# Two of sixteen attention-weight tiles of a unit made by GpSimd instead of VectorE, in a four-layer graph network

## The chip, the cores and the metric

The kernel runs on one core of one Trainium2 chip. The metric is the device time of one execution in microseconds (us), of which the median over runs is given. The engines are named as the profile names them: PE is TensorE (matrix products), DVE is VectorE, ACT is ScalarE, POOL is GpSimd, and SP is the queue from which most transfers (DMAs) are issued.

## The reference

Eight graphs (`x`: 8 x 2048 nodes x 64 features) share one adjacency matrix `adj` of 2048 x 2048. Four layers follow one another, each inside a residual with a layer norm. The first three are graph attention:

```
h   = x @ W                      # layer 0 has a layer norm and node weights ahead of it
s1  = h @ a[:64];  s2 = h @ a[64:]
e   = leaky_relu(s1[i] + s2[j], slope 0.2)
att = softmax over j of e, where adj[i, j] > 0
x   = layernorm(x + act(att @ h))      # act: elu in layers 0 and 1, relu in layer 2
```

Layer 3 is a softmax over neighbours for each feature and has no share in the change.

## The kernel before, in words

**Units.** The work of one layer on one graph is a unit. Line 1328 fixes the order: layer 0 of graphs 0 to 3, layer 1 of graphs 0 to 3, then the same for graphs 4 to 7, and then layer 2 of all eight. So units 0 to 15 belong to the first two layers. The text numbers units in that order.

**Tiles.** A unit has 16 tiles, one for every 128 source nodes j. A tile `w` has 128 partitions (j) and 2048 columns (all target nodes i), in float32. In layers 0 and 1 the exponential of the leaky score needs no ScalarE: with e^(0.8 s1[i]) as a row `r` over i and e^(-0.8 s2[j]) as a column `e[:, 1]`, the tile is

```
w[:, sl] = max(r[:, sl], low[:, jb]) * edge[:, jb, sl]
```

which is one VectorE instruction (`weights`, line 920). `edge` is the mask, kept in SBUF as FP8. `r` is the same row on all 128 partitions. Unit 0 has it in SBUF. For all later units TensorE spreads it into PSUM (`spread`, line 767) from three bfloat16 pieces `r3`, since PSUM holds one `r` only: the next unit's `r` can be written when VectorE has read the last tile of the present one. The first and last tile of such a unit are made in two halves.

`products` (line 969) multiplies each tile by the values `v` of its 128 nodes, four matmuls of 512 columns (two instructions each), and sums into PSUM over the 16 tiles. There are four `w` buffers, and one set of sums, which ScalarE copies out (`oT`) at the end of a unit.

**Order.** The loop over units and their 16 tiles is written out. Everything on TensorE, VectorE, ScalarE and GpSimd keeps program order (`InOrder`, line 70), and each engine executes its own queue strictly in that order. At tile (step) jb of a unit the loop emits: the weights (`reach`, line 949), the products, from step 10 on what prepares the next unit (`prepare`, line 747), and one step of each background generator (`Streams`, line 1294). Transfers are ordered by the framework's planner, and SP issues them one after the other.

**Background work.** While unit n runs, generators finish the unit before it and prepare later ones:

- `finish` (line 988) normalizes the sums (`den`, `p_o`), adds `hb` on GpSimd in layer 0 (called `o+hb` below), takes the elu on ScalarE, adds on GpSimd `eh<-eh,x` (`eh`) and `o<-o,eh` (`o+eh`), and then takes the statistics of the layer norm: `stats` (line 508) emits on VectorE the reduces `st_x<-o` and, two steps later, `st_x<-sq_x`; a power on GpSimd follows. At the earliest the first reduce is emitted at step 11 after a layer 0 unit and at step 9 after a layer 1 unit; `o+eh` is emitted two steps before it, `eh` three. Waits for PSUM slots can push all of these later.
- `scores` (line 698) and `features0` (line 608) make the scores of later units. Both end in `rows_term` (line 589): ScalarE copies the 8 KB row into `rT`, GpSimd splits it into three bfloat16 pieces with three casts and two in-place subtractions, and SP writes them to DRAM. `prepare` reads them back as `r3`, and multiplies `v` on GpSimd (`pv`).
- `mask_out` (line 310) widens the mask to float32 on ScalarE (`mf`, 32 copies, one every two steps from step 4 to 14, in units 9 to 14), and each copy is written to DRAM in a transfer of 512 KB. It uses four buffers, those of the integer mask's loads before it.

Of the kernel before, what the change touches and what calls it, by code (L numbers as in the profile page):

```python
# [8 lines left out]
F32 = mybir.dt.float32  # L9
F32R = mybir.dt.float32r  # L10
BF16 = mybir.dt.bfloat16
U8 = mybir.dt.uint8
FP8 = mybir.dt.float8e4
I32 = mybir.dt.int32
AF = mybir.ActivationFunctionType
ALU = mybir.AluOpType
AX = mybir.AxisListType

P = 128
# [31 lines left out]
def gnn4_kernel(ctx: ExitStack, tc: tile.TileContext, t, out):  # L51
    nc = tc.nc
    x_in, adjT = t["x"], t["adjT"]
    B, N, F = x_in.shape
    K = N // P
    K2 = K // 2
# [50 lines left out]
    class Banks:  # L107
# [7 lines left out]
        @classmethod  # L115
        def use(cls, name, bufs):
            if cls.stack is not None:
                cls.stack.close()
            cls.stack = ExitStack()
            cls.pool = cls.stack.enter_context(tc.tile_pool(name=name, bufs=bufs, space=PSUM))  # L120
# [139 lines left out]
    half_ldeg = consts.tile([P, K], F32, name="half_ldeg")  # L260
    raws = {}

    AT_W = (0, 1, 2, 3, 6, 7, 8, 9)

    def load_raw(jb):

        if jb in AT_W:
            r = work.tile([P, N], I32, tag="w", name=f"raw_{jb}", bufs=4)
            nc.sync.dma_start(r, adjT[jb * P : (jb + 1) * P])
            raws[jb] = [r[:, : N // 2], r[:, N // 2 :]]  # L270
        elif jb < K:
            raws[jb] = []
            for h in range(2):
                r = early.tile([P, N // 2], I32, tag="raw", name=f"raw_{jb}_{h}", bufs=4)
                nc.sync.dma_start(
                    r, adjT[jb * P : (jb + 1) * P, h * (N // 2) : (h + 1) * (N // 2)]
                )
                raws[jb].append(r)
# [31 lines left out]
    def mask_out():  # L310

        for jb in range(K):
            for h in range(2):
                while not 3 < now[2] < K - 1:
                    yield 1
                r = early.tile([P, K2, P], F32, tag="raw", name=f"mf_{jb}_{h}", bufs=4)
                act.copy(
                    r,
                    edge[:, jb, h * (N // 2) : (h + 1) * (N // 2)].rearrange(
                        "p (i c) -> p i c", c=P  # L320
                    ),
                )
                nc.sync.dma_start(
                    mask_d[h * K2 : (h + 1) * K2, :, jb].rearrange("i p c -> p i c"), r
                )
                yield 2
# [262 lines left out]
    def rows_term(sc, p, n, layer, b):  # L589

        if in_psum(layer, b):
            r = small.tile([K, P], F32, tag="rT", name=f"rT_{n}", bufs=1)
            act.copy(r, p)
            r3 = small.tile([K, 3, P], BF16, tag="rT3", name=f"rT3_{n}", bufs=1)
            for i in range(3):
                pool.tensor_copy(r3[:, i], r)
                if i < 2:
                    pool.tensor_tensor(r, r, r3[:, i], ALU.subtract)
            sc.row = dram.tile([3, K, P], BF16, tag="row3_d", name=f"row3_d_{n}", bufs=B + 1)
            nc.sync.dma_start(sc.row.rearrange("m k p -> k m p"), r3)  # L600
            return
        rT = small.tile([K, P], F32, tag="rT", name=f"rT_{n}", bufs=1)
        act.copy(rT, p)
        sc.row = dram.tile([K, P], F32, tag="row_d", name=f"row_d_{n}", bufs=B + 1)

        (nc.scalar if n == "0_0" else nc.sync).dma_start(sc.row, rT)
# [140 lines left out]
    def prepare(layer, b):  # L747

        n = f"{layer}_{b}"
        sc = S[layer, b]  # L750
        if in_psum(layer, b):
            sc.r3 = work.tile([P, 2 * N], BF16, tag="row", name=f"row3_{n}")[:3, :N]
            nc.sync.dma_start(sc.r3, sc.row.rearrange("m k p -> m (k p)"))
            if layer == 2:
                sc.v = V[layer, b].v
                return
            sc.v = early.tile([P, K, F], F32, tag="pv", name=f"pv_{n}", bufs=2)
            pool.tensor_tensor(sc.v, V[layer, b].v, bc_f(sc.e[:, 2]), ALU.mult)
            return
        sc.r = work.tile([P, N], F32, tag="row", name=f"row_{n}")  # L760
        (nc.scalar if n == "0_0" else nc.sync).dma_start(
            sc.r, bass.AP(tensor=sc.row.tensor, offset=sc.row.offset, ap=[[0, P], [1, N]])
        )
        sc.v = early.tile([P, K, F], F32, tag="pv", name=f"pv_{n}", bufs=2)
        pool.tensor_tensor(sc.v, V[layer, b].v, bc_f(sc.e[:, 2]), ALU.mult)

    def spread(layer, b):
# [148 lines left out]
    def halves(u, jb):  # L916
        parts = 2 if jb in (0, K - 1) and in_psum(u.layer, u.b) else 1
        return [slice(c * (N // parts), (c + 1) * (N // parts)) for c in range(parts)]

    def weights(u, jb):  # L920

        s = u.s
        w = u.w[jb] = work.tile([P, N], F32, tag="w", name=f"w_{u.n}_{jb}", bufs=4)
        low = s.low if u.layer == 2 else s.e[:, 1]
        for sl in halves(u, jb):
            dve.scalar_tensor_tensor(
                w[:, sl], s.r[:, sl], low[:, jb : jb + 1], edge[:, jb, sl], ALU.max, ALU.mult
            )
# [20 lines left out]
    def reach(t):  # L949

        while front[0] < K * len(todo):
            n, jb = divmod(front[0], K)
            layer, b = todo[n]
            if n not in prepared or front[0] > t + (2 if layer == 2 else 0):
                break
            if jb == 0:
                spread_for(n)
                units.append(unit(layer, b))
            weights(units[n], jb)
            front[0] += 1  # L960
            if jb == K - 1 and n + 1 in prepared:
                spread_for(n + 1)
        while behind[0] < min(front[0], t + 2):
            n, jb = divmod(behind[0], K)
            if todo[n][0] == 2:
                exponential(units[n], jb)
            behind[0] += 1

    def products(u, jb):

        s, w = u.s, u.w[jb]
        sums = [u.acc[c // 2][F * (c % 2) : F * (c % 2) + F, :] for c in range(NCH)]
        for c in range(NCH):
            pe.matmul(
                sums[c],
                lhsT=s.v[:, jb, :],
                rhs=w[:, c * 512 : (c + 1) * 512],
                start=(jb == 0),
                stop=False,
            )  # L980
        if jb == K - 1:

            assert s.whole
            for c in range(NCH):
                rows = slice(32 * c, 32 * c + 3)
                pe.matmul(sums[c], lhsT=s.mean[rows], rhs=emptyT[rows], start=False, stop=True)
# [384 lines left out]
    begin = {0: 2, 1: 3, 4: 4, 5: 5, 6: 6, 8: 7}  # L1371
    for n, (layer, b) in enumerate(todo):
        if (layer, b) == (2, 1):
            early_.close()
            late = ctx.enter_context(tc.tile_pool(name="late", bufs=1))
            bg.add(l3_products())
# [6 lines left out]
        for jb in range(K):  # L1383
            if n == 0:
                while masks < min(K, 9 + jb):
                    mask(p_deg, masks)
                    masks += 1
                    if masks == K:
                        empties(p_deg)
            now[2] = jb  # L1390
            reach(K * n + jb)
            u = units[n]
            if jb == 0:
# [539 lines left out]
```

## Time and profile before

| what | value |
|---|---|
| median of 3 runs | 1438.56 us (1435.73 to 1440.45) |
| profiled execution, its own time | 1439.37 us |
| its span | 1437.6 us |
| granted TensorE clock, mean | 0.945 |
| span from the end of unit 0 (115.7 us) to that of unit 15 (784.3 us) | 668.6 us |

The span runs from the first to the last instruction in the trace; times in the trace count from its start. In a group of instructions, "out<-in" names the tiles, "x" the number of instructions, then follow the busy time, the mean in ns, and the idle time of the engine just before them with what ended it. In a list of waits the three numbers are the total, the count and the longest. In a timeline the first two numbers are the start and the duration in us; a group in brackets is the idle time before, and what ended it. All instructions of the in-order engines carry the line of the recording helper (L80), so they are told apart by tile. Busy time of TensorE includes modelled ends.

### The profile page before, as it was taken

What the parts mean: (1) busy time and instruction counts of PE and PEld (TensorE: products, weight loads), DVE (VectorE), ACT (ScalarE), POOL (GpSimd) and SP (SyncE); (2) the same over time, 40 slices, a digit from 0 to 9 for tenths busy, and PEclk for the clock granted to TensorE, in tenths of its full rate; (3) what the DMA queues carried; (4) which work ended last, traced back from release to release, by engine and by line L of the source; (5) the groups of instructions that cost most, each with busy time, mean ns of one, the idle gap of its engine ahead of it and who ended that gap; (6) DMA issues with size and microseconds to landing.
All of it is one profiled execution on the core that took longest, in us unless ns stands there. A gap on an engine that the chain in (4) does not pass through costs nothing.

```text
span 1437.6 us, 19117 instructions
## 1 busy us (share of the span) xinstructions
PE 1238.5 (86%) x7138; PEld 620.0 (43%) x7138; DVE 1260.6 (88%) x1260; ACT 820.3 (57%) x1585; POOL 548.0 (38%) x619
## 2 busy tenths in 40 slices
PE   3578788988899988999998887879999898988996
PEld 2323233333233333344332332336665464647996
DVE  4699889997899999999999898898989988878976
ACT  4415444664557545654533986787677766675442
POOL 1152463324423344331322211312445534367665
PEclk9988999999999999999999897999999998989998
DMA  8740000000000022221201000005453354531111
GB/s 297 249 81 1 1 2 1 1 2 1 3 1 1 22 69 88 89 75 53 68 16 37 1 1 15 12 26 150 130 155 101 108 152 116 141 97 46 38 37 33
DMA packets 113335, 90.36 MB, mean 63 GB/s; under 512 B 58077, under 2 KB 91021, under 8 KB 112082
## 3 DMA queue, kind: packets, MB, share of 16 engines
q1 hardware_dynamic: 112690, 87.89, 20.9%
q8 instruction: 58, 0.95, 0.3%
q10 hardware_dynamic: 544, 1.17, 0.2%
q14 instruction: 43, 0.35, 0.1%
HBM read 63.54 MB, written 25.46 MB: 62 GB/s over the span
## 4 chain that ended last, share of the span: by engine, by line
PE 28%; DVE 20%; ACT 8%; issue 5%; POOL 3%; DMA 1%; SPq 0%; POOLq 0%; DVEq 0%; ACTq 0%
PE p_l L80 13%; DVE w L80 12%; PE acc L80 12%; ACT w L80 3%; DVE st_x L80 2%; ACT x L80 2%; DVE o L80 1%; PE p_o L80 1%; ACT sp L80 1%; POOL o L80 1%; PE r L80 1%; DMA mask<-mask_d 1%; DVE x L80 1%; DVE nd L80 1%; DVE fs L80 1%
## 5 line engine op out<-in xcount | busy, mean ns | idle before, releaser
L80 DVE SCALAR_TENSOR_TENSOR w<-r,se,edge 128x2048 f32<-128x2048 f32 (+1 forms) x270 | 555.4, 2103 | 22.0 <-PE r L80 19.2
L80 PE MATMUL acc<-w,pv 128*64 128x512 f32 x2048 | 508.9, 629 | 70.8 <-DVE w L80 63.9
L80 DVE SCALAR_TENSOR_TENSOR w<-r,lo_g,edge 128x2048 f32<-128x2048 f32 (+1 forms) x144 | 298.0, 2095 | 18.1 <-PE r L80 9.7
L80 PE MATMUL acc<-w,x 128*64 128x512 f32 x1024 | 269.1, 656 | 37.0 <-ACT w L80 33.0
L80 ACT ACTIVATE w<-w,down_g 128x2048 f32<-128x2048 f32 (+1 forms) x144 | 257.3, 1809 | 71.2 <-DVE w L80 70.7
L80 PEld LDWEIGHTS p_l<-v,mask 128*128 128x128 f32 x2048 | 253.0, 193 | 65.4 <-issue 52.3
L80 PEld LDWEIGHTS acc<-w,pv 128*64 128x64 f32 x2048 | 133.5, 141 | 337.3 <-issue 190.2
L80 PE MATMUL p_l<-v,mask 128*128 128x256 f32 x2048 | 269.1, 289 | 9.8 <-POOL mask L80 6.3
L80 PEld LDWEIGHTS acc<-w,x 128*64 128x64 f32 x1024 | 68.2, 146 | 163.5 <-issue 92.2
L80 ACT COPY oT<-acc 128x512 f32<-128x512 f32 x48 | 25.8, 589 | 147.5 <-PE acc L80 147.5
L80 ACT ACTIVATE x<-o,st_x 128x64 f32<-128x64 f32 x256 | 90.5, 444 | 1.4 <-DVE st_x L80 1.4
L80 ACT ACTIVATE o<-p_o,den 128x64 f32<-128x64 f32 x256 | 55.9, 326 | 44.9 <-DVE den L80 44.9
L80 ACT ACTIVATE nd<-p_l,empty 128x256 f32<-128x256 f32 x64 | 30.2, 471 | 82.5 <-PE p_l L80 82.4
L80 POOL TENSOR_SCALAR isw_x<-isw_x 128x16 f32<-128x16 f32 x24 | 6.2, 260 | 182.6 <-DVE isw_x L80 171.1
L80 POOL TENSOR_TENSOR st_x<-isw_x,mhalf 128x16 f32<-128x16 f32 x24 | 70.3, 2930 | 2.0
L80 PEld LDWEIGHTS p_o<-rh,oT 128*128 128x128 f32 x384 | 49.7, 196 | 35.9 <-issue 15.4
L80 POOL TENSOR_TENSOR st_h<-isw_h,mhalf 128x16 f32<-128x16 f32 x8 | 23.6, 2952 | 106.7 <-DVE isw_h L80 83.8
L80 PE MATMUL p_o<-rh,oT 128*128 128x130 f32 x384 | 59.9, 293 | 4.6 <-ACT o L80 3.5
L80 DVE RECIPROCAL nd<-nd 128x256 f32<-128x256 f32 x32 | 55.8, 1743 | 0.0
L80 POOL TENSOR_TENSOR eh<-eh,x 128x1024 f32<-128x1024 f32 (+2 forms) x24 | 36.4, 1532 | 45.3 <-ACT eh L80 45.2
L80 POOL COPY x<-x 128x16 f32<-128x16 f32 x16 | 3.3, 205 | 123.8 <-ACT x L80 123.8
L80 PE MATMUL r<-row,ones 3*128 3x512 bf16 x92 | 26.9, 416 | 24.7 <-DVE w L80 23.6
(243 smaller groups left out, 1497.4 us busy)
## 6 DMA issues: line engine op xcount, KB each, us to landing
mask<-mask_d SPq DMA_DIRECT2D x140, 256.0 KB
mask_d<-mf SPq DMA_DIRECT2D x32, 512.0 KB
raw<-in_adjT_dram SPq DMA_DIRECT2D x8, 1024.0 KB
raw<-in_adjT_dram SPq DMA_DIRECT2D x16, 512.0 KB
x<-in_x_dram SPq DMA_DIRECT2D x8, 512.0 KB
x_d<-x SPq DMA_DIRECT2D x8, 512.0 KB
e<-x_d SPq DMA_DIRECT2D x64, 64.0 KB
out_dram<-o SPq DMA_DIRECT2D x64, 64.0 KB
```

The source lines that it names most:

```text
L80: ins = f(*args, **kwargs)
```

## The change

For units 1 to 15, tiles 6 and 12 (`ASIDE`) are no longer made by VectorE. GpSimd makes each in four pieces of 512 columns (`aside`): a tensor_scalar with two maxima, and a multiply by the mask. One piece is emitted at the start of each of steps 1 to 4 (tile 6) and 7 to 10 (tile 12), five tiles ahead. `products` takes the pieces in place of the columns of `w`. There are four piece buffers (`off`), so a piece of tile 12 reuses the buffer of tile 6's piece of the same number.

[...]`rows_term` also writes `rT` in float32 to DRAM (8 KB), ahead of GpSimd's split, and `prepare` reads it back onto all 128 partitions (`rowf`, 1 MB, one buffer).

Memory for this comes from three places. The integer mask's buffers move to a pool of their own, closed at step 8 of unit 0, and a pool "stage" takes their place. `mf` gets one buffer there instead of four. The values `v` of units 1 to 15 move from the pool "early" to the second half of the row tile whose first half holds `r3`.

```diff
--- before.py
+++ after.py
@@ -260,6 +260,18 @@
     half_ldeg = consts.tile([P, K], F32, name="half_ldeg")
     raws = {}
 
+    class Stage:
+        stack = ExitStack()
+        pool = None
+
+        @classmethod
+        def use(cls, name):
+            cls.stack.close()
+            if name:
+                cls.pool = cls.stack.enter_context(tc.tile_pool(name=name, bufs=1))
+
+    Stage.use("raws")
+
     AT_W = (0, 1, 2, 3, 6, 7, 8, 9)
 
     def load_raw(jb):
@@ -271,7 +283,7 @@
         elif jb < K:
             raws[jb] = []
             for h in range(2):
-                r = early.tile([P, N // 2], I32, tag="raw", name=f"raw_{jb}_{h}", bufs=4)
+                r = Stage.pool.tile([P, N // 2], I32, tag="raw", name=f"raw_{jb}_{h}", bufs=4)
                 nc.sync.dma_start(
                     r, adjT[jb * P : (jb + 1) * P, h * (N // 2) : (h + 1) * (N // 2)]
                 )
@@ -313,7 +325,7 @@
             for h in range(2):
                 while not 3 < now[2] < K - 1:
                     yield 1
-                r = early.tile([P, K2, P], F32, tag="raw", name=f"mf_{jb}_{h}", bufs=4)
+                r = Stage.pool.tile([P, K2, P], F32, tag="mf", name=f"mf_{jb}_{h}", bufs=1)
                 act.copy(
                     r,
                     edge[:, jb, h * (N // 2) : (h + 1) * (N // 2)].rearrange(
@@ -591,6 +603,8 @@
         if in_psum(layer, b):
             r = small.tile([K, P], F32, tag="rT", name=f"rT_{n}", bufs=1)
             act.copy(r, p)
+            sc.rowf_d = dram.tile([K, P], F32, tag="row_d", name=f"rowf_d_{n}", bufs=B + 1)
+            nc.sync.dma_start(sc.rowf_d, r)
             r3 = small.tile([K, 3, P], BF16, tag="rT3", name=f"rT3_{n}", bufs=1)
             for i in range(3):
                 pool.tensor_copy(r3[:, i], r)
@@ -749,19 +763,25 @@
         n = f"{layer}_{b}"
         sc = S[layer, b]
         if in_psum(layer, b):
-            sc.r3 = work.tile([P, 2 * N], BF16, tag="row", name=f"row3_{n}")[:3, :N]
+            both = work.tile([P, 2 * N], BF16, tag="row", name=f"row3_{n}")
+            sc.r3 = both[:3, :N]
             nc.sync.dma_start(sc.r3, sc.row.rearrange("m k p -> m (k p)"))
             if layer == 2:
                 sc.v = V[layer, b].v
                 return
-            sc.v = early.tile([P, K, F], F32, tag="pv", name=f"pv_{n}", bufs=2)
+            sc.rowf = Stage.pool.tile([P, N], F32, tag="rowf", name=f"rowf_{n}")
+            nc.sync.dma_start(
+                sc.rowf,
+                bass.AP(tensor=sc.rowf_d.tensor, offset=sc.rowf_d.offset, ap=[[0, P], [1, N]]),
+            )
+            sc.v = both[:, N:].bitcast(F32).rearrange("p (k f) -> p k f", k=K)
             pool.tensor_tensor(sc.v, V[layer, b].v, bc_f(sc.e[:, 2]), ALU.mult)
             return
         sc.r = work.tile([P, N], F32, tag="row", name=f"row_{n}")
         (nc.scalar if n == "0_0" else nc.sync).dma_start(
             sc.r, bass.AP(tensor=sc.row.tensor, offset=sc.row.offset, ap=[[0, P], [1, N]])
         )
-        sc.v = early.tile([P, K, F], F32, tag="pv", name=f"pv_{n}", bufs=2)
+        sc.v = early.tile([P, K, F], F32, tag="pv", name=f"pv_{n}", bufs=1)
         pool.tensor_tensor(sc.v, V[layer, b].v, bc_f(sc.e[:, 2]), ALU.mult)
 
     def spread(layer, b):
@@ -917,6 +937,21 @@
         parts = 2 if jb in (0, K - 1) and in_psum(u.layer, u.b) else 1
         return [slice(c * (N // parts), (c + 1) * (N // parts)) for c in range(parts)]
 
+    ASIDE = (6, 12)
+
+    def aside(u, jb, c):
+
+        s = u.s
+        sl = slice(c * 512, (c + 1) * 512)
+        y = Stage.pool.tile([P, 512], F32, tag="off", name=f"off_{u.n}_{jb}_{c}", bufs=NCH)
+        e = s.e[:, 1, jb : jb + 1]
+        pool.tensor_scalar(y, s.rowf[:, sl], e, e, ALU.max, ALU.max)
+        pool.tensor_tensor(y, y, edge[:, jb, sl], ALU.mult)
+        u.w.setdefault(jb, []).append(y)
+
+    def set_aside(n):
+        return todo[n][0] < 2 and n > 0
+
     def weights(u, jb):
 
         s = u.s
@@ -956,7 +991,12 @@
             if jb == 0:
                 spread_for(n)
                 units.append(unit(layer, b))
-            weights(units[n], jb)
+            if set_aside(n):
+                for later_jb in ASIDE:
+                    if 0 <= jb - later_jb + 5 < NCH:
+                        aside(units[n], later_jb, jb - later_jb + 5)
+            if not (set_aside(n) and jb in ASIDE):
+                weights(units[n], jb)
             front[0] += 1
             if jb == K - 1 and n + 1 in prepared:
                 spread_for(n + 1)
@@ -974,7 +1014,7 @@
             pe.matmul(
                 sums[c],
                 lhsT=s.v[:, jb, :],
-                rhs=w[:, c * 512 : (c + 1) * 512],
+                rhs=w[c] if isinstance(w, list) else w[:, c * 512 : (c + 1) * 512],
                 start=(jb == 0),
                 stop=False,
             )
@@ -1371,6 +1411,7 @@
     begin = {0: 2, 1: 3, 4: 4, 5: 5, 6: 6, 8: 7}
     for n, (layer, b) in enumerate(todo):
         if (layer, b) == (2, 1):
+            Stage.use(None)
             early_.close()
             late = ctx.enter_context(tc.tile_pool(name="late", bufs=1))
             bg.add(l3_products())
@@ -1388,6 +1429,8 @@
                     if masks == K:
                         empties(p_deg)
             now[2] = jb
+            if n == 0 and jb == 8:
+                Stage.use("stage")
             reach(K * n + jb)
             u = units[n]
             if jb == 0:
```

## The prediction

> **What bounds the kernel now.** The change touches only the first two layers, so I read the page for the engine shares first, then cut the span at the end of each unit (the copy of its sums out of PSUM). Unit 0 ends at 115.7 us and unit 15 at 784.3. The page, and then the sum over those fifteen windows:
>
> ```profile
> PE 1238.5 (86%) x7138; PEld 620.0 (43%) x7138; DVE 1260.6 (88%) x1260; ACT 820.3 (57%) x1585; POOL 548.0 (38%) x619
> ```
> ```profile
> sum 668.60, PE 600.39 PEld 231.81 DVE 619.73 ACT 346.72 POOL 246.88; mean PE 40.03 PEld 15.45 DVE 41.32 ACT 23.11 POOL 16.46
> ```
>
> A unit takes 44.6 us on average: VectorE is busy for 41.3 of it, TensorE for 40.0, GpSimd for 16.5. The two busiest are almost level, so work taken from VectorE is worth at most TensorE's idle time, 668.6 - 600.4 = 68 us, and GpSimd has room on average. The groups of instructions in this stretch give the prices (the last line is of the whole span):
>
> ```profile
> L80 DVE SCALAR_TENSOR_TENSOR w<-r,se,edge 128x2048 f32<-128x2048 f32 x210 | 482.2, 2339 | 0.8 <-PE acc L80 0.8
> L80 POOL TENSOR_TENSOR pv<-x,se 128x1024 f32<-128x1024 f32 x8 | 15.2, 1902 | 0.0
> L80 POOL TENSOR_TENSOR h<-y 128x512 f32<-128x512 f32 x6 | 7.6, 1274 | 0.5
> L80 POOL CAST mask<-edge 128x2048 fp32r<-128x2048 fp8e4 x15 | 29.0, 1934 | 19.6 <-PE p_l L80 19.6
> ```
>
> An average hides where the slow units lose their time. VectorE's waits name it: it waits for the row matmuls at unit boundaries, and for GpSimd's `o`.
>
> ```profile
> DVE w L80 <- PE r L80: 20.3, 12, 6.2
> DVE st_x L80 <- POOL o L80: 14.5, 5, 5.2
> ```
>
> Unit 1 in order of time, from the engines' timelines, shows what such a wait costs:
>
> ```profile
> 149.72 1.94 PE L80 MATMUL acc<-w,pv 128*64 128x512 f32 x8 [0.32 <-DVE w L80]
> 157.34 1.86 PE L80 MATMUL r<-row,ones 3*128 3x512 bf16 x4 [5.68 <-DVE w L80]
> 159.13 3.68 PE L80 MATMUL acc<-w,pv 128*64 128x512 f32 x8
> ```
> ```profile
> 153.69 1.22 DVE L80 TENSOR_REDUCE st_x<-o 128x16 f32<-128x1024 f32 x1 [4.02 <-POOL o L80]
> ```
> ```profile
> 151.32 2.34 POOL L80 TENSOR_TENSOR o<-o,eh 128x1024 f32<-128x1024 f32 x1
> ```
>
> The reduce `st_x<-o` stands in VectorE's queue ahead of the unit's last weight tile. GpSimd ends `o` at 153.66, the reduce starts at 153.69, TensorE has idled 5.68 us by then and does its next tile in 3.68 us instead of 1.94. In eight of the fifteen units the reduce starts within 0.5 us of the end of `o`. So GpSimd, 37% busy here, is on the path through the second half of a unit.
>
> **What the Trainium skill says.** (1) "GPSIMD Engine Reference", section 3.1: bodies of up to two operations run at 1.03 cycles an element, two-input ones at about 2.6. The trace agrees: the cast's 1934 ns over 2048 elements, less the smaller casts' start-up, is 0.86 ns an element; the add of 512 takes 1274 ns. (2) "SBUF — State Buffer", section "SBUF: two separate sides": a VectorE operation with two SBUF inputs and a GpSimd one lock each other out for a whole instruction. It agrees: one `mean` update took 2.19 us at 232.46 instead of 0.27, under GpSimd's `eh` (232.22 to 234.57). Weight tiles read `r` from PSUM and never exceed 2.351 us. (3) "TensorE: Matmul & The Clock Gate", "Part 1: The HAM clock gate": the array runs at half rate after idling. The 3.68 us tile above agrees. (4) "DMA: Bandwidth & Descriptors", "Anatomy of one DMA — SWDGE (gpsimd) path": a transfer costs about 2 us before its bytes, there when issued by GpSimd. Here, issued by SP, a row's write goes out at 145.10 and the read that waits for it at 146.63, 1.5 us later.
>
> **The change part by part.**
>
> *Removed:* two full tiles a unit, 15 x 2 x 2.339 = 70 us of VectorE, 4.7 a unit.
>
> *Added on GpSimd:* eight pieces a unit, each a tensor_scalar and a multiply of 512. No row shows a wide tensor_scalar. Low bound: skill (1) gives an estimate of 0.44 us before start-up. High: the growth between GpSimd's 4- and 16-element tensor_scalars (234 and 260 ns, 2.2 ns an element) gives 1.35. I take 0.65, from the cast's slope plus 0.2. The multiply is 1.27 by the `h<-y` row; half of `pv` (0.95) is the low bound, since the FP8 operand is narrower. With gaps a piece is 2.05 (1.5 to 2.75), 16.4 a unit, so GpSimd goes to about 33 us of 44: no throughput bound.
>
> *Where they queue.* Tile 6's pieces come at steps 1 to 4, where GpSimd mostly idles: in unit 3 it is idle from 214.6 to 227.6, and four pieces (8.2) end near 223, before tile 6 at 225.6. Hidden. Tile 12's come at steps 7 to 10. They wait for tile 6's matmuls (four `off` buffers) and stand ahead of `o+hb`, `eh`, `pv` and `o+eh`, hence of the reduce. For each unit: pieces ahead of `o+eh` x 2.05, plus 1.6 for each row chain there, less GpSimd's idle time from tile 6 (0.6 us in) to the end of `o`, less the time that the reduce came after `o`. The number of pieces follows from the step of the reduce, read off the weight tiles left after it. Units 1 to 15, us late: 3.4, 1.5, 0.1, 3.5, 3.6, -1.2, 2.7, -1.6, 1.8, 3.1, 0.9, 1.1, 3.8, 0.6, -0.5. For unit 1: 8.2 + 1.6 - 6.4 idle - 0.0 = 3.4. In units 6, 8, 12, 14 and 15 the reduce comes by step 11, so the skipped tile 12 still follows and gives 2.3 back: -3.5, -3.3 (TensorE idles no more than 3.3 there), -1.2, -1.7, -2.8. Unit 2's 1.5 hides under the 6.2 us that VectorE then waits for `r`. Sum: 22.9 - 12.5 = +10. Skipping tile 6 lets the reciprocals before `o` start earlier: 2.3 at most, but they wait for `p_o` too; 0.5 for ten units, -5.
>
> The 4.7 us that VectorE gains before the reduce are thus not worth 4.7: it arrives earlier and waits.
>
> *Row chain.* GpSimd's in-place subtract on `rT` must now wait until the new 8 KB write has read it: 1.5 us as above, less a cast beside it, plus the issue (0.32): 1.6 (0 to 2.5). Behind it wait the row's own write and all of GpSimd. Only unit 7's boundary is tight (casts end 388.0, read 389.5, `r` waits until 391.15): +1.6. The others are in the sums above.
>
> *The broadcast.* 1 MB at the 250 to 297 GB/s that this trace reached is about 4 us, 6 with its latency. It waits for step 10's piece. Beside the boundary, over 10 us off, it is hidden; in unit 7 it lands near 399, and tile 6 is due at 412.
>
> *`mf` from four buffers to one.* Each copy on ScalarE now waits for the last one's 512 KB write: 0.36 issue, 2.1 data, 1.2 latency, 3.7 us. Copies are meant two steps (5.5 us) apart, but come in pairs when ScalarE is late (552.54, 603.14: two in 1.98 us), and one in six writes queues behind a 1 MB broadcast that itself waits at SP for GpSimd. ScalarE is half idle. I take 1.5 us for each of units 9 to 13 (0 to 3): +7.5.
>
> *Others.* `v` in the row tile: its buffer was freed a unit earlier, nothing. More locked small VectorE operations: some 86 of them, GpSimd two-input time up by 120 x 1.27 = 152 us of 669, so 86 x 0.23 x 0.6 = 12 us, ahead of a reduce that waits anyway: nothing. Two more tiles at half clock after the longer stalls: 2 x 1.7 = +3.4.
>
> Sum: 10 - 5 + 1.6 + 7.5 + 3.4 = +17.5 on the profiled execution's 1439.4, so 1456.9; the median is 0.8 lower: **1456 us**.
>
> **Rivals.** *Faster:* the pieces fit GpSimd's idle time, since they cost 1.5 us or ScalarE's parts arrive earlier by more than I allow. Then the reduce comes on time, VectorE's 4.7 us a unit show, and TensorE bounds at 40.0 plus some 2 us: 15 x 2.2 = 33 less, 1406. For: GpSimd is 63% idle, and units 14 and 15 have TensorE at 36.7 of 41. Against: `o` ends where the reduce begins in eight units. It decides where four pieces cost under about 5 us. *No change:* gains in the light units and losses in the heavy ones cancel, 1439; for it: my sum is a difference of terms as large as itself. *Much slower:* a tensor_scalar of 1.35 us makes a piece 2.75, 0.7 x 3.9 more in ten units = +27, or tile 12 itself is late: 1484. *The tiles don't leave VectorE:* excluded by the code.
>
> **How the numbers follow.** Forecast (1443 to 1475) 0.45, much slower 0.15, no change 0.14, faster 0.26. Faster by over 0.3% (what a measurement here can tell, 4.3 us): 0.26; same 0.14; slower 0.60. The piece's bounds move the forecast by -20 and +27, ScalarE's by 7; its own range is 1428 to 1488. Leaving 0.12 below and 0.08 above: 1418 to 1486.
>
> **What would show it.** Right: VectorE's weight tiles fall by 30, its waits for `o` rise from 14.5 us to 50 or more, GpSimd's busy time grows by some 245 us, `rT` waits for a DMA about 1.5 us fifteen times. Wrong: those waits stay below 20 us while TensorE's idle time falls (faster), or TensorE waits for `off` (tile 6 or 12 late), or a piece is far from 2.05.

## The result, and the profile after

| kernel | median | range | against before |
|---|---|---|---|
| before | 1439.35 us | 1435.73 to 1440.45 | |
| the change | 1551.29 us | 1550.36 to 1554.56 | 1.0787 [1.0761, 1.0812] |

The kernel became 112 us slower, where 17.5 were forecast. The direction was right, the size was not. The engine shares of the page after, and the sum over the fifteen windows from the end of unit 0 (110.3 us) to that of unit 15 (897.6 us):

```profile
PE 1279.5 (83%) x7138; PEld 634.5 (41%) x7138; DVE 1200.0 (77%) x1230; ACT 821.9 (53%) x1585; POOL 924.1 (60%) x859
```
```profile
sum 787.30, PE 643.86 PEld 247.08 DVE 566.21 ACT 349.58 POOL 623.79; mean PE 42.92 PEld 16.47 DVE 37.75 ACT 23.31 POOL 41.59
```

The copy that ends unit 15 in the kernel before starts at 785.7 us, not at 784.3 as the table above and the prediction have it, so the stage took 670.0 us there. Now it takes 787.3, 117.3 more, and that is all of the loss: unit 0 ended 5.4 us earlier, and the work after unit 15 took 0.5 us less. VectorE lost 60.6 us of busy time: 70 for the 30 weight tiles, less some 9 that its small instructions took longer. GpSimd gained 376, not 245: it is now as busy in this stage (41.6 us a unit of 52.5) as VectorE was before. TensorE's busy time rose by 43 us for the same 3068 matmuls, and its idle time by 74. The groups of the stage say what a piece costs (columns: count, busy time and mean in ns, idle time before and what ended it):

```profile
L80 POOL TENSOR_SCALAR off<-rowf,se 128x512 f32<-128x512 f32 x120 | 248.3, 2069 | 14.4 <-PE acc L80 14.4
L80 POOL TENSOR_TENSOR off<-off,edge 128x512 f32<-128x512 f32 x120 | 131.6, 1097 | 10.0
L80 PE MATMUL acc<-off,row 128*64 128x512 f32 x240 | 84.4, 663 | 44.7 <-POOL off L80 44.5
L80 DVE SCALAR_TENSOR_TENSOR w<-r,se,edge 128x2048 f32<-128x2048 f32 x180 | 413.9, 2338 | 0.0
L80 ACT CAST mf<-edge 128x1024 f32<-128x1024 fp8e4 x32 | 33.7, 1054 | 71.1 <-DMA mask_d<-mf 71.0
```

The tensor_scalar takes 2.07 us, where the prediction took 0.65 and allowed 1.35 at most. The multiply is 1.10, a little under its 1.27. With gaps a piece is 3.24 us (from 111.34 to 114.58 in unit 1), not 2.05. The list of waits of the stage shows who pays:

```profile
DVE st_x L80 <- POOL o L80: 139.3, 14, 15.6
ACT sq_x L80 <- POOL o L80: 81.9, 10, 13.6
ACT mf L80 <- DMA mask_d<-mf: 71.0, 19, 13.5
PE acc L80 <- POOL off L80: 44.5, 16, 6.0
DVE w L80 <- PE r L80: 36.9, 12, 10.4
```

VectorE's waits for `o` rose from 14.5 us to 139.3. TensorE waits for the pieces themselves, which before had no counterpart; nearly all of these waits are for tile 12's. Unit 1 again, from the timelines of GpSimd, TensorE and VectorE:

```profile
127.46 2.06 POOL L80 TENSOR_SCALAR off<-rowf,se 128x512 f32<-128x512 f32 x1 [3.16 <-PE acc L80]
130.67 2.93 POOL L80 TENSOR_TENSOR st_h<-isw_h,mhalf 128x16 f32<-128x16 f32 x1
136.84 2.37 POOL L80 TENSOR_TENSOR o<-o,hb 128x1024 f32<-128x1024 f32 x1
144.56 1.09 POOL L80 TENSOR_TENSOR off<-off,edge 128x512 f32<-128x512 f32 x1
153.22 2.34 POOL L80 TENSOR_TENSOR o<-o,eh 128x1024 f32<-128x1024 f32 x1
```
```profile
142.49 1.07 PE L80 MATMUL acc<-off,row 128*64 128x512 f32 x2 [2.73 <-POOL off L80]
159.25 1.86 PE L80 MATMUL r<-row,ones 3*128 3x512 bf16 x4 [7.69 <-DVE w L80]
161.04 3.68 PE L80 MATMUL acc<-w,row 128*64 128x512 f32 x8
```
```profile
155.59 1.22 DVE L80 TENSOR_REDUCE st_x<-o 128x16 f32<-128x1024 f32 x1 [14.17 <-POOL o L80]
```

The first piece of tile 12 waits 3.16 us for tile 6's matmuls to free the buffer. The other three stand between the power `st_h`, `o+hb` and `eh`, and the last ends at 145.65. `o` ends at 155.56, the reduce starts 0.03 us later after VectorE has idled 14.17 us, and the next unit's `r` follows at 159.25. Before, the same `r` came at 157.34 in a unit that had begun 5.4 us later: 7.3 us were lost in this unit.

### The profile page after: what moved, and what is told of

It is laid out like the page before. It is cut to its first block, busy times and chain, and to the rows that moved or that the text cites. A ratio compares the mean times of both kernels' runs of the same rounds, so it can differ in the third digit from the quotient of the medians.

```text
span 1548.9 us, 19379 instructions
## 1 busy us (share of the span) xinstructions
PE 1279.5 (83%) x7138; PEld 634.5 (41%) x7138; DVE 1200.0 (77%) x1230; ACT 821.9 (53%) x1585; POOL 924.1 (60%) x859
## 4 chain that ended last, share of the span: by engine, by line
PE 21%; DVE 14%; POOL 10%; ACT 8%; DMA 2%; issue 2%; SPq 0%; POOLq 0%; DVEq 0%; ACTq 0%
PE p_l L80 11%; PE acc L80 8%; DVE w L80 7%; POOL off L80 5%; ACT w L80 3%; POOL o L80 2%; ACT x L80 1%; DVE o L80 1%; DVE st_x L80 1%; POOL st_x L80 1%; DMA mask_d<-mf 1%; ACT sp L80 1%; DVE x L80 1%; PE p_o L80 1%; PE r L80 1%
## 5 line engine op out<-in xcount | busy, mean ns | idle before, releaser
L80 DVE SCALAR_TENSOR_TENSOR w<-r,se,edge 128x2048 f32<-128x2048 f32 (+1 forms) x240 | 487.2, 2073 | 38.8 <-PE r L80 36.8
L80 PE MATMUL acc<-w,row 128*64 128x512 f32 x1680 | 437.4, 648 | 48.2 <-DVE w L80 41.9
L80 POOL TENSOR_SCALAR off<-rowf,se 128x512 f32<-128x512 f32 x120 | 248.3, 2069 | 14.4 <-PE acc L80 14.4
L80 PEld LDWEIGHTS acc<-w,row 128*64 128x64 f32 x1680 | 117.9, 145 | 272.7 <-issue 172.4
L80 POOL TENSOR_TENSOR off<-off,edge 128x512 f32<-128x512 f32 x120 | 131.6, 1097 | 10.0
L80 DVE TENSOR_REDUCE st_x<-o 128x16 f32<-128x1024 f32 x24 | 29.2, 1215 | 139.3 <-POOL o L80 139.3
L80 PE MATMUL acc<-off,row 128*64 128x512 f32 x240 | 84.4, 663 | 44.7 <-POOL off L80 44.5
L80 ACT ACTIVATE sq_x<-o 128x1024 f32<-128x1024 f32 x24 | 25.4, 1057 | 87.0 <-POOL o L80 81.9
L80 ACT CAST mf<-edge 128x1024 f32<-128x1024 fp8e4 x32 | 33.7, 1054 | 71.1 <-DMA mask_d<-mf 71.0
```

The source lines that it names most:

```text
L80: ins = f(*args, **kwargs)
```

## The experiments

Where nothing else is said, a run is measured against the kernel before on the same chip. "Above the plumbing" means above the run that has the change's memory moves and row, but no pieces. What a run gains by relieving VectorE is already in such a difference.

**What GpSimd's operations cost.** The kernel before, with eleven kinds of instruction three times over at its end, when the other engines are done.

```diff
+        pool.tensor_scalar(y_, x_, c_, c_, ALU.max, ALU.max)
+        pool.tensor_scalar(y_, x_, c_, c_, ALU.mult, ALU.add)
+        pool.tensor_tensor(y_, x_, c_.to_broadcast([P, 512]), ALU.mult)
...
```

> The kernel before with 36 GpSimd instructions added at its end, on idle engines; their results are unused. It prices each form at 128x512 float32: copy, tensor_scalar with an immediate or a per-partition column, one operation or two, maximum or multiply, and tensor_tensor with a broadcast column. My theory (the maximum is what is dear): about 0.6 us for the copy, 0.6 to 0.7 for a multiply, 1.0 to 1.1 for one maximum and 2.07 for two. Rival (the column operand is dear): 2.07 with a column whatever the operation, 0.6 with an immediate. Rival (waiting or port contention in the changed kernel made it 2.07): 0.65 here.

The timeline of GpSimd, one instruction of each kind: a copy; a maximum with a constant, two maxima with constants, one maximum with a column, two maxima with columns, a multiply and add with columns; multiply and add of a broadcast column as tensor_tensor; a multiply by a constant; a multiply by the FP8 mask.

```profile
1435.85 0.61 POOL L80 COPY pr_b<-pr_a 128x512 f32<-128x512 f32 x1
1436.55 1.50 POOL L80 TENSOR_SCALAR pr_b<-pr_a 128x512 f32<-128x512 f32 x1
1438.13 1.93 POOL L80 TENSOR_SCALAR pr_b<-pr_a 128x512 f32<-128x512 f32 x1
1440.16 1.56 POOL L80 TENSOR_SCALAR pr_b<-pr_a,pr_e 128x512 f32<-128x512 f32 x1
1441.82 2.08 POOL L80 TENSOR_SCALAR pr_b<-pr_a,pr_e 128x512 f32<-128x512 f32 x1
1443.99 0.77 POOL L80 TENSOR_SCALAR pr_b<-pr_a,pr_e 128x512 f32<-128x512 f32 x1
1444.85 1.04 POOL L80 TENSOR_TENSOR pr_b<-pr_a,pr_e 128x512 f32<-128x512 f32 x1
1445.96 1.04 POOL L80 TENSOR_TENSOR pr_b<-pr_a,pr_e 128x512 f32<-128x512 f32 x1
1447.09 1.50 POOL L80 TENSOR_SCALAR pr_b<-pr_a 128x512 f32<-128x512 f32 x1
1448.68 1.09 POOL L80 TENSOR_TENSOR pr_b<-pr_b,edge 128x512 f32<-128x512 f32 x1
```

The two maxima cost 2.08 us on an idle chip too, so the price is the instruction's own and not contention. A tensor_scalar is 1.5 to 2.1 us for 512 elements in all forms tried but one, multiply and add, at 0.77. Neither the maximum (a multiply alone costs 1.50 as well) nor the column (a constant saves 0.1) makes it dear by itself; what does was not found.

**The plumbing alone.** No tile is set aside; the float32 row, its broadcast and the memory moves stay.

```diff
-    ASIDE = (6, 12)
+    ASIDE = ()
```

> The changed kernel with no tile set aside: all 16 tiles on VectorE, but the row's second write, the 1 MB broadcast, v in the row tile and mf's one buffer stay. My theory (the pieces carry the loss): the row chain's 1.6 and mf's 7.5 us of the prediction, less the 5 us that unit 0 gained: 1435 to 1455 us. Rival (the plumbing carries it, since ScalarE waited 71 us for mask writes after the change): 1490 us or more.

Measured: 1452.88 us against 1435.64, ratio 1.0104 [1.0075, 1.0133]: 17 us, for which the prediction had 1.6 + 7.5. Unit 6 alone lost 7.7 us, at its end, where TensorE waits for the next unit's row. SP's timeline there (start, duration, line of issue):

```profile
386.87 0.30 SPq L607 DMA_DIRECT2D rowf_d<-rT  x1
388.20 0.34 SPq L773 DMA_DIRECT2D rowf<-rowf_d  x1
389.95 0.32 SPq L614 DMA_DIRECT2D row_d<-rT  x1
392.91 0.34 SPq L773 DMA_DIRECT2D rowf<-rowf_d  x1
393.36 0.24 SPq L768 DMA_DIRECT2D row<-row_d  x1
397.54 0.34 SPq L773 DMA_DIRECT2D rowf<-rowf_d  x1
```

and TensorE's:

```profile
397.58 1.88 PE L80 MATMUL r<-row,ones 3*128 3x512 bf16 x4 [6.65 <-DMA row<-row_d]
```

The row `r3` is written at 389.95 and could be read some 1.5 us later, as in the kernel before. Its read is issued only at 393.36, right behind a second broadcast, which itself was issued 4.7 us after the first, into the same single buffer. The 12 KB land some 4 us later, beside that second 1 MB; `r` follows at 397.58, where it came at 391.15 before.

**Tile 6 alone.** The pieces at steps 1 to 4 only.

```diff
-    ASIDE = (6, 12)
+    ASIDE = (6,)
```

> The changed kernel with tile 6 alone set aside; tile 12 goes back to VectorE. My theory (the pieces ahead of o+eh carry the loss, and only tile 12's stand there): near the kernel with no tile set aside, 1430 to 1460 us, with VectorE's waits for o below 40 us. Rival (any piece work on GpSimd delays the finish chain, about half each): 1490 to 1505 us.

Measured: 1460.02 us, ratio 1.0155 [1.0128, 1.0181], 7 above the plumbing. The time is at the upper edge of the range expected. VectorE's waits for `o` came to 48.6 us, more than the 40 expected; it arrives earlier and waits.

**A piece at the predicted price.** The maximum is replaced by a multiply with the column, as a tensor_tensor (1.04 us instead of 2.07), so the weights of both tiles are products instead of maxima. A piece is then some 2.2 us.

```diff
-        pool.tensor_scalar(y, s.rowf[:, sl], e, e, ALU.max, ALU.max)
+        pool.tensor_tensor(y, s.rowf[:, sl], e.to_broadcast([P, 512]), ALU.mult)
```

> The changed kernel with the maximum replaced by a tensor_tensor multiply with the broadcast column, so that the attention weights are the product instead of the maximum and the result is not the reference's. A piece then costs about 0.95 + 1.1 = 2.05 us, the price that the prediction used, and everything else is as in the changed kernel. My theory (only the size of one term was wrong): 1445 to 1480 us. Rival (the mechanism is wrong too: late tiles on TensorE and mf's one buffer cost what the prediction left out): 1500 us or more.

Measured: 1487.89 us, ratio 1.0358 [1.0336, 1.0380], between the two ranges expected: 52 us slower than before and 35 above the plumbing. So the wrong price is some 60 of the 112 us, and at the right price the forecast would still have missed 35.

The split is approximate, since this run changes more than the length of a piece. Its tensor_tensor has two inputs where the tensor_scalar has one, and VectorE's small instructions took longer beside it: in unit 3 `st_x<-st_x` took 0.93 us at 220.08, while such a piece ran from 219.95 to 220.99, where it takes 0.16 before and 0.38 in the change. VectorE's busy time in the stage is 576.0 us, against 566.2 in the change, for the same tiles. So part of the 35 may belong to this form; how much was not tried.

**One maximum.** The same values with one maximum instead of two equal ones; a piece is 2.7 us.

```diff
-        pool.tensor_scalar(y, s.rowf[:, sl], e, e, ALU.max, ALU.max)
+        pool.tensor_scalar(y, s.rowf[:, sl], e, None, ALU.max)
```

> The change with one maximum in place of two equal ones in the tensor_scalar (the same values): measured alone at 1.57 instead of 2.08 us, so a piece of some 2.75 us where the change has 3.24 and the run with the broadcast multiply 2.2. If the length of a piece sets the loss, the time lies between those two runs (1488 and 1551), near 1520 (1505 to 1535), and VectorE's waits for o between 86 and 139 us. If GpSimd is late by a whole slot whatever the piece costs, it stays within 10 us of 1551. The prediction's own rival named 1484 for a piece of 2.75; I expect that to be exceeded.

Measured: 1515.16 us against 1437.48, ratio 1.0552 [1.0517, 1.0588], waits for `o` 118.1 us. This lies in the range expected if the length of a piece sets the loss. Against before, the three lengths 2.2, 2.7 and 3.2 us cost 52, 78 and 112 us: for these pieces in this place, each 0.1 us of a piece is some 5 to 7 us of the kernel. Sixty pieces paid in full would give 6, and tile 12 has sixty. The line through the two forms of the maximum alone would give an estimate of 44 us at 2.2, less than the 52 of the run with two inputs.

**Tile 12 alone.**

```diff
-    ASIDE = (6, 12)
+    ASIDE = (12,)
```

> Only tile 12 is given to GpSimd (four pieces a unit, with the plumbing); tile 6 stays with VectorE. Theory A, its place in the queue: its pieces stand ahead of o+hb, eh and o+eh at steps 7 to 10, and that alone is what costs; then the run keeps nearly all of the loss, 1515 to 1545 us, with VectorE waiting for o for over 110 us. Theory B, the coupling of the two tiles: with both, tile 12's pieces can't start before the matmuls of tile 6 have freed the four piece buffers; with tile 12 alone the buffers are free early, GpSimd runs ahead through the stretch that it otherwise idles in, and the run takes 1460 to 1490 us, waits for o below 80 us. I lean to B. If load alone counted, the two tiles alone (this and tile 6 alone, +7 over the plumbing) would add up to the whole change; under B they fall well short of it.

Measured: 1524.20 us, ratio 1.0609 [1.0577, 1.0640]: 87 us slower, some 70 above the plumbing. Theory B, to which I leaned, fell: the free buffers hardly help. (VectorE's waits for `o` are 97.8 us, less than the 110 that theory A named.) GpSimd's timeline in unit 3 shows why:

```profile
219.81 2.08 POOL L80 TENSOR_SCALAR off<-rowf,se 128x512 f32<-128x512 f32 x1
221.97 1.10 POOL L80 TENSOR_TENSOR off<-off,edge 128x512 f32<-128x512 f32 x1
232.75 2.37 POOL L80 TENSOR_TENSOR o<-o,hb 128x1024 f32<-128x1024 f32 x1 [9.67 <-ACT o L80]
235.09 2.08 POOL L80 TENSOR_SCALAR off<-rowf,se 128x512 f32<-128x512 f32 x1
244.04 1.10 POOL L80 TENSOR_TENSOR off<-off,edge 128x512 f32<-128x512 f32 x1
249.39 2.34 POOL L80 TENSOR_TENSOR o<-o,eh 128x1024 f32<-128x1024 f32 x1
```

The first piece uses the idle stretch. The second could run at 223.07, but it stands behind `o+hb`, which waits 9.67 us for ScalarE. Three pieces then come between `o+hb` and `eh`. The two tiles alone cost 7 and 70 us above the plumbing, together 77, and with the change 95: some 18 come from having both. The 14.4 us that GpSimd waits for tile 6's matmuls may be part of it; that was not tried.

**Tile 12 alone, in another place.** The same sixty pieces at steps 1 to 4.

```diff
-                    if 0 <= jb - later_jb + 5 < NCH:
-                        aside(units[n], later_jb, jb - later_jb + 5)
+                    if 0 <= jb - later_jb + 11 < NCH:
+                        aside(units[n], later_jb, jb - later_jb + 11)
```

> Tile 12 alone, as before (1524, 71 above the plumbing), but its four pieces are emitted at steps 1 to 4, eleven tiles ahead, instead of 7 to 10: the same sixty pieces at the same price, in another place of GpSimd's queue. If the place decides (at steps 7 to 10 the pieces stand behind instructions that wait for VectorE and ScalarE, and ahead of o): close to tile 6 alone, 1456 to 1472 us, VectorE's waits for o below 60 us and hardly any wait of TensorE for off. If the load decides (13 us a unit on GpSimd, or its lock on VectorE's operands): 1500 us or more.

Measured: 1455.92 us against 1437.77, ratio 1.0109 [1.0069, 1.0149]. The same work at the same price costs nothing above the plumbing, the relief of VectorE taken off. In units 1 to 8, where no mask is written, the pieces at steps 7 to 10 lost 44 us against the kernel before, and these 4. GpSimd's timeline of unit 3 in this run:

```profile
213.41 2.08 POOL L80 TENSOR_SCALAR off<-rowf,se 128x512 f32<-128x512 f32 x1
225.26 1.10 POOL L80 TENSOR_TENSOR off<-off,edge 128x512 f32<-128x512 f32 x1
226.56 2.37 POOL L80 TENSOR_TENSOR o<-o,hb 128x1024 f32<-128x1024 f32 x1 [0.19 <-ACT o L80]
235.00 2.35 POOL L80 TENSOR_TENSOR o<-o,eh 128x1024 f32<-128x1024 f32 x1 [1.46 <-ACT o L80]
```

All four pieces fill the stretch in which GpSimd idled 12.95 us before `o+hb` in the kernel before. From the end of `o+hb` to that of `o+eh` it takes 8.4 us here and in the kernel before, and 16.6 with the pieces at steps 7 to 10. The load is the same, so it is the place in GpSimd's queue that decides.

**What the relief is worth.** The kernel before, with tiles 6 and 12 of units 1 to 15 made by nobody: their products read a constant.

```diff
-            weights(units[n], jb)
+            if not (todo[n][0] < 2 and n > 0 and jb in (6, 12)):
+                weights(units[n], jb)
...
-                rhs=w[:, c * 512 : (c + 1) * 512],
+                rhs=ones[:, None, :].to_broadcast([P, 4, P]) if w is None else w[:, c * 512 : (c + 1) * 512],
```

> The kernel before, with tiles 6 and 12 of units 1 to 15 made by nobody: the products of those two tiles read a constant instead, so the result is not the reference's. It shows the most that taking the two tiles off VectorE can bring, with no cost put anywhere else. If the relief counts as the prediction's faster rival has it (VectorE is the bound and TensorE follows at about 42 us a unit): 1400 to 1412 us. If VectorE only arrives earlier at its waits for GpSimd's o and for r: 1418 to 1430 us, with those waits grown by 20 us or more.

Measured: 1412.25 us against 1437.48, ratio 0.9817 [0.9789, 0.9845]. The time falls between the two ranges expected. With nothing added elsewhere the 70 us of VectorE are worth 25 here, 1.7 a unit of 4.7. In the list of waits VectorE now waits 38.9 us for `o`, 24 more than before, with GpSimd's work unchanged:

```profile
DVE st_x L80 <- POOL o L80: 38.9, 10, 7.7
```

**Which part of the plumbing.** First the memory moves alone, then with the row's write but no broadcast.

```diff
-            sc.rowf_d = dram.tile([K, P], F32, tag="row_d", name=f"rowf_d_{n}", bufs=B + 1)
-            nc.sync.dma_start(sc.rowf_d, r)
...
-            sc.rowf = Stage.pool.tile([P, N], F32, tag="rowf", name=f"rowf_{n}")
-            nc.sync.dma_start(
...
```

> The kernel before with only the memory moves of the change: mf with one buffer, the values v in the row tile; no float32 row is written or broadcast, no piece is made. The plumbing with the row cost 17 us. If mf is most of it: 1445 to 1452 us here, ScalarE waiting for its writes for some 25 us or more. If the row's write and broadcast are most of it (the broadcast stands ahead of the small row's read on SP): 1436 to 1442 us. I expect between, 1443 (1438 to 1448): the units 9 to 13 as in the run with all the plumbing, unit 6 without its 7.7 us.

Measured: 1440.52 us, ratio 1.0026 [1.0006, 1.0047]: 3 us. ScalarE waits 26.6 us for its writes, and little of it counts.

```diff
-            sc.rowf = Stage.pool.tile([P, N], F32, tag="rowf", name=f"rowf_{n}")
-            nc.sync.dma_start(
...
```

> The plumbing without the broadcast: the float32 row is still written to DRAM, ahead of GpSimd's split, but not read back onto the partitions; no piece is made. All the plumbing took 1452.9, the memory moves alone 1440.5. If the 1 MB broadcasts on SP's queue are the cost: 1439 to 1446 us, and the boundary after unit 6 as before. If GpSimd's wait for the row's write is (about 1.2 us fifteen times): 1448 to 1454. I expect the first, 1444.

Measured: 1439.70 us, ratio 1.0014 [0.9996, 1.0033]. The write of the row, and GpSimd's wait for it, cost nothing that can be measured. What remains of the 17 us, some 14, is the broadcast.

**The broadcast on another queue.** The plumbing with the fifteen broadcasts issued by ScalarE in its program order.

```diff
-            nc.sync.dma_start(
+            act.dma_start(
                 sc.rowf,
```

> The plumbing alone (1452.9 with the broadcasts on SP's queue, 1439.7 without them), with the fifteen 1 MB broadcasts issued by ScalarE, in its program order, instead of SP. If their place on SP's queue is the cost (the small row's read and the mask's writes stand behind them): 1438 to 1445 us. If their bytes are (they still compete with the same reads and writes for the DMA engines): 1449 to 1456. I lean to the first, 0.6; after unit 6 three broadcasts follow one another at 388.2, 392.9 and 397.5, each waiting for the one before, with the row's read issued between them at 393.4.

Measured: 1443.67 us, ratio 1.0044 [1.0029, 1.0059]: 5 us in place of 17, with the same bytes. So most of the broadcast's cost is its place on SP's queue, ahead of small transfers that somebody waits for. The bytes seem to cost something too: unit 6 is still 4.6 us longer than before in this run. The 12 KB row is written at 387.01, beside a broadcast issued at 385.27, and its read can be issued only at 390.31, 3.3 us later instead of 1.4. The same edit in the run with tile 12's pieces at steps 1 to 4:

> Tile 12 alone with its pieces at steps 1 to 4 (1455.9), with the broadcasts issued by ScalarE instead of SP. Its units 1 to 8 were 3.7 us and its units 9 to 13 24.5 us longer than before, all of that where broadcasts and mask writes share SP's queue. If that queue is the cost: 1430 to 1442 us, ScalarE's waits for the mask's writes back from 54 to under 30 us, and the relief of VectorE (12 us for one tile at most) begins to show. If not: 1450 us or more.

Measured: 1434.89 us against 1438.27, ratio 0.9983 [0.9966, 1.0000]. Before this edit units 9 to 13 were 24.5 us longer than in the kernel before, with it 7.4; the waits of ScalarE for the mask's writes fell as well, from the first to the second of these lists:

```profile
ACT mf L80 <- DMA mask_d<-mf: 54.0, 19, 11.3
```
```profile
ACT mf L80 <- DMA mask_d<-mf: 36.0, 16, 5.4
```

They stayed above the 30 us expected, the time within the range. The Trainium skill ("Trainium Kernel Development and Optimization", "Key Constraints") says that issuing transfers from several engines only saves issue time. Here it saved 12 us in the plumbing and 21 with the pieces: an instruction on SP's queue that waits holds all those behind it.

This bears on the change as well. The broadcast into the single buffer waits there until GpSimd has made its last piece from it; SP's waits in the change:

```profile
SPq L773 <- POOL off L80: 211.9, 12, 36.3
```

Units 9 to 13, where the mask's writes stand behind it, lost 10.0 us each, the eight units before them 7.9. What part of the change's loss is this queue and not GpSimd's was not tried: the change with its broadcasts issued by ScalarE is a run that is missing.

**ScalarE's help.** Tile 6 alone; ScalarE makes relu(r - e) from the row in PSUM, GpSimd adds e in the 0.77 us form and multiplies by the mask; no float32 row, three `mf` buffers.

```diff
-        pool.tensor_scalar(y, s.rowf[:, sl], e, e, ALU.max, ALU.max)
+        act.activation(y, s.r[:, sl], AF.Relu, bias=s.e[:, 3, jb : jb + 1])
+        pool.tensor_scalar(y, y, ones[:, :1], e, ALU.mult, ALU.add)
```

> A try at a faster kernel. Only tile 6 leaves VectorE. ScalarE makes relu(r - e) of a piece from the row in PSUM, GpSimd adds e to it (one times x plus a column, 0.77 us by the price run) and multiplies by the mask (1.1), so a piece is 1.9 us on GpSimd, at steps 1 to 4; no float32 row and no broadcast, three mf buffers. Most that one tile can bring is half of the 25 us that leaving two tiles unmade brought. If GpSimd's early steps are free and ScalarE's four pieces (some 0.7 us each) are too: 1424 to 1432 us. If ScalarE's share delays the copies of the sums or the elu, or GpSimd is late with o again: 1436 to 1450. I give the first 0.45.

Measured: 1504.92 us against 1437.77, ratio 1.0453 [1.0414, 1.0493], outside both ranges. GpSimd is hardly later with `o` than before (VectorE waits 21.9 us for it, 14.5 before); whether ScalarE's other work was late was not looked into. The list of waits names a reason that I had not thought of.

```profile
POOL off L80 <- ACT off L80: 110.7, 41, 13.6
DVE w L80 <- ACT off L80: 82.3, 56, 4.2
```

VectorE only reads `r`, as ScalarE does, and yet waits for ScalarE's read; in the trace none of ScalarE's 60 reads of the PSUM row overlaps with one of VectorE's, and they follow one another in the order in which they are emitted. So VectorE is held by ScalarE's queue at four tiles a unit. Whether the framework's dependences or the chip ask for this was not tried.

**A form that is faster.** Tile 12 alone, pieces at steps 1 to 4, broadcasts by ScalarE, one maximum.

```diff
-        pool.tensor_scalar(y, s.rowf[:, sl], e, e, ALU.max, ALU.max)
+        pool.tensor_scalar(y, s.rowf[:, sl], e, None, ALU.max)
```

> Tile 12 alone, pieces at steps 1 to 4, broadcasts issued by ScalarE (1434.9), and one maximum instead of two equal ones, so a piece of 2.7 us instead of 3.2: GpSimd is done 2 us earlier in a unit. If the length of the pieces still counts in this place (VectorE waits 39 us for o, 14.5 before): 1427 to 1433 us, those waits near 30. If only the place did: 1434 to 1437. I give the first 0.55.

Measured: 1431.44 us against 1437.28, ratio 0.9960 [0.9943, 0.9976]: 6 us (0.4%) faster than before, and in the first range expected. VectorE's waits for `o` did not fall as expected with it: 37.6 us in the traced execution, the slowest of the run's 22, against 39.0 with two maxima. Against the form with two maxima (0.9983 [0.9966, 1.0000]) the intervals overlap, so what the shorter piece brings here is not settled. It is small beside what it brings at steps 7 to 10: half a microsecond off each piece is 3 us here by the ratios, and 34 there, with both tiles and so twice as many pieces.

## Why the prediction was wrong

*What bounds the kernel* held. GpSimd's `o` ahead of the reduce sets the second half of a unit. (A reading was off: the 5.68 us of TensorE's idle time in unit 1 end at 157.34, when the tile after the reduce is made, and not at 153.69.) The run with the tiles unmade shows the same from the other side: relieving VectorE by 70 us brings 25, since it "arrives earlier and waits".

*The price of a piece* is the largest error. "I take 0.65, from the cast's slope plus 0.2" stood for 2.07, and the high bound of 1.35 was too low. The low bound followed the Trainium skill ("GPSIMD Engine Reference", 3.1), whose 1.03 cycles an element for bodies of up to two operations would give an estimate of 0.44 us; the trace differs, at 4.0 ns an element, and the measurement decides. The growth between the two smallest tensor_scalars, 2.2 ns an element, did not carry over either: at 128 columns the two maxima took 0.80 us in the price run, so 3.3 ns an element from there to 512. The cast was the wrong neighbour: a one-input copy takes 0.61 us where the tensor_scalar takes 2.08. From the change and the run at the predicted price, this is 112 - 52 = 60 of the 95 us missed, perhaps more, since that run's form may have a cost of its own. The prediction's own sum agrees: 1.19 us more a piece, for its 3.9 pieces in ten to fifteen units, makes an estimate of 46 to 70. The rival *much slower* had the right mechanism and both its signs ("or tile 12 itself is late"), but with 2.75 as its dearest piece it ended at 1484; a piece of that length measured 1515.

*Where they queue* is the second error, 27 us by the medians. At its own price the prediction put pieces, reciprocals and half clock at 10 - 5 + 3.4 = 8.4 us; the run with pieces of 2.2 us shows 35 above the plumbing. (In the traces the fifteen units lost 24 against it: the plumbing's traced execution was 6 us above its median, and the rest lies outside these units.) The step that failed is "less GpSimd's idle time from tile 6 (0.6 us in) to the end of `o`". It took the time of tile 6 from the kernel before, and counted all of GpSimd's idle time from then on as room. Unit 3 of that run has it plainest, in the timelines of VectorE and GpSimd:

```profile
216.87 1.03 DVE L80 SCALAR_TENSOR_TENSOR mean<-mean,later,mean 128x64 f32<-128x64 bf16 x1
220.08 0.93 DVE L80 SCALAR_TENSOR_TENSOR st_x<-st_x 128x16 f32<-128x16 f32 x1
```
```profile
229.16 1.04 POOL L80 TENSOR_TENSOR off<-rowf,se 128x512 f32<-128x512 f32 x1 [4.83 <-PE acc L80]
231.33 2.38 POOL L80 TENSOR_TENSOR o<-o,hb 128x1024 f32<-128x1024 f32 x1
```

While tile 6's pieces are made, these two small instructions take 1.03 and 0.93 us, 0.25 and 0.16 before. Tile 6's matmuls start 23.9 us into the unit, 22.1 before. GpSimd idles 4.83 us until they free a buffer, and `o+hb`, which stands behind that piece, starts 27.2 us into the unit, 24.0 before: the idle time counted ahead of it is gone. `o` ends 8.2 us later in the unit, where the formula has 5.3 (0.1, since the reduce came 5.2 after `o`), and the unit loses 4.4 above the plumbing. In units 7 and 10 tile 6 is 2 us and more later as well, and `o` 8.0 and 6.8 later, where the formula has 5.2 and 3.1. So the "locked small VectorE operations", put at 12 us of work and "nothing" of time, are not nothing: in this unit they are 1.6 of the 1.8 us that tile 6 is late, for they stand ahead of the matmuls that free the buffers. Over the stage they took some 20 us more than before in this run and some 9 in the change; what they cost there was not measured. For units 1, 4 and 5 the formula was near: 3.4, 3.5 and 3.6 forecast, 2.2, 4.4 and 4.6 lost. Units 12 and 14 lost some 4 us more than forecast each, the 2.3 of the skipped tile among them; why was not looked into.

*Tile 6 hidden* held nearly: 7 us above the plumbing even at 3.2 us a piece. *Half clock*, forecast at 3.4 us, was too small at the true length of the waits: TensorE's busy time in the stage rose by 43 us at a granted clock of 0.89 instead of 0.96. This is part of how the waits are paid, and no further cost beside the runs' differences.

*The broadcast* was called hidden, and cost some 14 us. The prediction looked only at when its own data are due, and not at what stands behind it on SP; with one buffer for it, a second broadcast waits there for the first, and the 12 KB row behind both. *Row chain*: the waits of `rT` are there (10 times, 10.6 us), about 1 us each, and are worth nothing measurable, against 1.6. *`mf` in one buffer* was forecast at 7.5 and is 3 alone; it becomes dearer where broadcasts stand ahead of its writes. In all the plumbing is 17 instead of 9, the third error, 8 us. With pieces to wait for, the broadcast holds SP longer, and what that adds is not shown.

The three errors are 60 + 27 + 8 = 95 us, the difference of 112 and 17.5; they add up by construction, and the border between the first two is approximate. The marks named for "wrong" were the right ones: TensorE waits for `off` (44.5 us), and a piece is far from 2.05.

## What to carry to other kernels

Before work goes to an engine that looks idle, find whose wait its idle time is: in a queue kept in order only what is emitted ahead of the waiting instruction can use it, and what is emitted behind it delays whoever waits next (the same sixty pieces cost 70 us above the plumbing at steps 7 to 10 and nothing at steps 1 to 4). Measure the exact form of an operation on the engine that is to run it, and don't price it by a neighbour. A large transfer in a shared issue queue is costed by what stands behind it, not by when its own data are due.

## What was unexpected of the hardware

On GpSimd, 512 float32 elements on each of 128 partitions took 0.61 us as a copy, 0.77 as a tensor_scalar with multiply and add by columns, 1.04 to 1.10 as a two-input tensor_tensor (a broadcast column or the FP8 mask as second input), and 1.50 to 2.08 as any other tensor_scalar tried: the one-input operation was dearer than the two-input one. One maximum instead of two equal ones saves 0.5 us. What VectorE feels of it differs by form, which point (2) of the prediction does not tell apart: in the change, 12 of the 16 `mean` updates that began under a tensor_scalar took 0.25 to 0.28 us as on an idle GpSimd, and the nine under the multiply by the mask 0.29 to 1.13. And two engines' reads of one row in PSUM came one after the other in this program, which cost VectorE 82 us of waits.
